# A four-layer graph network on one core: making the first elements and the matrix of the order statistics while the attention ends, moving the transposes of its result, and taking one product off VectorE

## The chip, the core and the metric

The kernel runs on one core of a Trainium2 chip. A core has five engines that run their own instruction streams: TensorE for matrix products (PE in the profile, with its weight loads as PEld), VectorE (DVE), ScalarE (ACT), GpSimd (POOL) and SyncE (SP). SP, ACT and POOL also issue the transfers between the device's memory and the core's on-chip memory, SBUF. Products land in PSUM, a second on-chip memory of eight banks. Times are device microseconds (us) of one execution.

## The reference: four layers over sixteen graphs

The input is `x`, 16 graphs x 1024 nodes x 64 channels, an adjacency matrix `adj` of 1024 x 1024 per graph, and a node mask. Four layers follow each other; after each the layer's input is added and a layer norm over the channels taken:

```
x = layernorm(x + L0(x, adj))   # degree-normalized product with adj, leaky relu
x = layernorm(x + L1(x, adj))   # attention, 8 heads, scores plus gated adj
x = layernorm(x + L2(x, adj))   # order statistics over neighbours, then an MLP
x = layernorm(x + L3(x, adj))   # adj @ (x @ W) + b
```

Layer 2 is the unusual one. Each node keeps a pruned list of its neighbours, and for each of the 64 channels it needs the neighbours' values at the quantiles 0.25, 0.5 and 0.75 (interpolated between two ranks and weighted):

```
nd   = adj_d > 0                                    # pruned neighbours
vals = where(nd[..., None], x[:, None, :, :], inf)
s    = sort(vals, axis=2);  nv = nd.sum(2)
for tau, w in zip((0.25, 0.5, 0.75), (0.25, 0.5, 0.25)):
    pos = tau * max(nv - 1, 0);  lo, hi = floor(pos), ceil(pos)
    agg = agg + w * (s[lo] + (pos - lo) * (s[hi] - s[lo]))
y = relu((x + agg) @ W1 + b1) @ W2 + b2
```

## The kernel before

**Turns.** The graphs go in eight pairs; the two graphs' 64 channels together fill the 128 partitions. The main loop (L1205) has nine turns. Turn p holds, in this order:

1. Layer 0 of both graphs of pair p (`layer0`, L402), which also finds the pruned neighbours and stores them as a mask in the device's memory (`nd_d`). Between the two graphs stand the last two layers of pair p-2 (`ends`, L1193, which calls `layers23`, L1029).
2. The attention of pair p (`attention`, L471): 64 steps of scores, exponentials, transposes and weighted sums, limited by TensorE, and at the end the projections of the heads (L562) with normalizations. The result `x2` is stored (L644), transposed on TensorE (L649), copied by ScalarE (L650) and stored again as `x2T` (L651).
3. A sort of pair p-1, beside the attention (`middle`, which calls `sort`). Every channel's 1024 values are sorted by a bitonic network of 55 steps. A forward step is three VectorE instructions, a comparison and two exchanges (all recorded as L1117), and a store of the comparison's mask. A backward pass replays the masks and yields every node's rank; `words_of` (L1079) turns ranks into three small numbers for each node and channel (`rk`, `u_w`, `b_w`). The swaps are written at step 58 of the attention. The last backward ones are paced, each behind an instruction of the attention; the forward ones have no such bond.
4. The order statistics of pair p-1 (`quantiles`, L788). VectorE makes *elements* E from those numbers (`words`, L767 to L785): a power of two for each node, by the rank. TensorE multiplies them with the neighbour matrix `ndT` (`half_word`, L849), so that a *word* V holds, as bits, which ranks occur among the neighbours, and sums of them. A group of 4 channels needs three words of 1024 columns, each made as two halves of eight matmuls, one bank a half, which ScalarE copies out (L857). There are 16 such groups per graph. Then come 96 steps, one for every group and quantile of both graphs: a comparison on VectorE (L862), a one-hot of the block (L871), a pick of the word at that block (L880, two of 1.75 us a step, the largest item on VectorE) and its sum on TensorE. Each eight steps make a *unit*, whose picked words are searched for the k-th set bit by a chain of short dependent VectorE instructions (`kth_bit`, L694 to L763). The found positions then select values (`distances`, `least_values`, `sum_values`), and a product with the interpolation's weights (L929) ends the unit, with a store of its result (L930). After the last step come the last search and a tail, mostly on TensorE, for the last unit.

Turn 0 has no sort and no order statistics. Turn 8 has neither layer 0 nor attention: the last layers of pair 6, the sort and the order statistics of pair 7. The last layers of pair 7 follow.

**What sets the order.** A scheduler ("planner" below) orders each engine's instructions ahead of time. It goes by the order in which the program is written as priority, and it gives a free engine any instruction that is ready by its estimates. A chain written out in the program (`then`, `product`) fixes the order of TensorE's matmuls in the attention and after the first words; some instructions (`behind`) are tied to others by hand. VectorE's stream has no such chain over the stages, so instructions of one stage can stand between those of another.

**Space.** SBUF is handed out in pools, from the left end or from the right end of a partition. A pool's tiles can only be written when the tiles that lay at that place before have been used for the last time. Beside the attention, the left end holds its data (`nat`, `att`), and the right end the sort's: `keys` at bytes 217056 to 229344 and `srt` at 201376 to 217056. The order statistics have three pools, `kb`, `qe` and `qn`, from byte 33088 up to 229088, so they lie over both the attention's and the sort's space. The elements, the matrix, `lim`, `V`, `lt` and `m` are in `qe`; the results and values (`vals`) in `qn`. The next turn's keys (L1169, loaded from `x2T`) lie at the right end again.

**The seams.** The matrix of the first graph is loaded by eight transfers on SP at the head of the order statistics, and there the first six elements are made, ahead of the first two groups' words, whose matmuls are outside the written-out chain.

Of the kernel before, what the change touches and what calls it, by code (L numbers as in the profile page):

```python
# [13 lines left out]
F32 = mybir.dt.float32  # L14
# [11 lines left out]
P = 128  # L26
N = 1024
# [83 lines left out]
def gnn_kernel(ctx: ExitStack, tc: tile.TileContext, a: dict, out: bass.AP):  # L111
# [100 lines left out]
    def bank(shape, dtype=F32):  # L212
        return ps1.tile(shape, dtype, name="bank")
# [257 lines left out]
    def attention(nat, ip, graphs, wqkv, x2, beside):  # L471

# [3 lines left out]
        with (tc.tile_pool(name="att", bufs=2, reuse_waits="tile") as att,  # L476
# [120 lines left out]
            for st, (gr, hp, nh, k4) in enumerate(steps):  # L597
                at = 8 * hp + 4 * nh + k4
                if k4 % 2 == 0:
                    pT = [[att1.tile([P, 4, 256], F32, name="pT", bufs=8) for mh in range(2)] for h in range(2)]  # L600
                scores_of(st + 1)
                if at == 2:
                    values(gr, 3)
                transposes(exps.pop(st), pT, k4 % 2)
                exponentials(exps.get(st + 1, ()))

                next(parts, None)
                if at == 0:
                    for _ in parts:
                        pass  # L610
                if k4 % 2:
                    for _ in parts:
                        pass
                    parts = weighted(gr, hp, 2 * nh + k4 // 2, pT)
                if at == 1:
                    for k in range(3):
                        values(gr, k)
                if gr is g1 and 2 <= at < 6:
                    heads(g0, at - 2)
                if st == BESIDE:  # L620
# [21 lines left out]
            for k in range(2, 4):  # L642
                heads(g1, k)
            nc.gpsimd.dma_start(x2_d[ds(ip * P, P)], x2)  # L644
            x2T = att1.tile([P, N], F32, name="t_pr")
            for hf in range(2):
                ps = bank([P, 4, P])
# [137 lines left out]
                nc.vector.tensor_tensor(Ev[w], Ev[1], over_t(b_w[w]), ALU.mult)  # L785
        return E

    def quantiles(ip, rk, u_w, b_w):  # L788

# [11 lines left out]
        with ExitStack() as es:  # L801
# [5 lines left out]
            class Graph(SimpleNamespace):  # L807
                pass

            graphs = [Graph(bb=bb, r=slice(bb * C, (bb + 1) * C), bd={}, base={}, V={}, E={}) for bb in range(2)]  # L810

            def load_matrix(gr):
                gr.ndT = qe.tile([P, NB, N], F8, name="ndT", bufs=2)
                for k in range(NB):
                    nc.sync.dma_start(gr.ndT[:, k, :].bitcast(U8), nd_d[gr.bb][ds(ip * P, P), k, :])
# [29 lines left out]

            def product(*args, **kw):
                then(nc.tensor.matmul(*args, **kw))  # L847

            def half_word(gr, g, w, hf, matmul):  # L849

# [71 lines left out]
            def sum_values(u, s):  # L922
                gr, g, q = u.pairs[s]
                for t in range(4):
                    product(u.acc[32 * t:32 * t + 32, :], bonesf[:, s, :], u.vals[s][t],
                            start=False, stop=(s == U8N - 1), tile_position=(0, 32 * t))
                if s == U8N - 1:
                    res = qn.tile([P, 512], F32, name="vals", bufs=5)
                    nc.vector.tensor_tensor(res, u.acc, gr.cf[u.n % 3], ALU.mult)  # L929
                    nc.gpsimd.dma_start(agg_d[gr.bb][:, u.n, :], res)  # L930

            picked = None
# [6 lines left out]
            todo = [(k, ws) for k in range(len(groups)) for ws in ([0], [1, 2])]  # L939
            made = used = 0  # L940

            def elements():

                nonlocal made
                k, ws = todo.pop(0)
                gr, g = groups[k]
                gr.E.setdefault(g, []).extend(words(qe, gr.bb * G + g, ws, rk, u_w, b_w))
                made += len(ws)

            def more_elements():  # L950
# [251 lines left out]

    for p in range(B // 2 + 1):  # L1205
        with double_banks(), ExitStack() as es:
            if p >= 1:
                keys = es.enter_context(tc.tile_pool(name="keys", bufs=1, reuse_waits="tile", side="right"))
                key = sort_keys(keys, p - 1)
            last = ends(p - 2) if p >= 2 else iter(())  # L1210
            if p < B // 2:
                nat = es.enter_context(tc.tile_pool(name="nat", bufs=1, reuse_waits="tile"))
                x2 = nat.tile([P, NB, 2, C], F32, name="x2")
                graphs = [Graph(bb=bb, x1=nat.tile(NODES, F32, name=f"x1_{bb}")) for bb in range(2)]
                adj = [nat.tile([P, N], F32, name=f"adj{k}") for k in range(NB)]
                wqkv = twice(nat, "wqkv", a["WqkvT"], 3 * H * C)
                with tc.tile_pool(name="l0", bufs=1, reuse_waits="tile") as l0:
                    tables = place_tables(l0)
                    for gr in graphs:
                        gr.adj = list(adj)  # L1220
                        layer0(l0, tables, p, gr.bb, None if gr.bb else adj, gr.x1)
                        if gr.bb == 0:
                            for part in (keys_of, gates, queries_of):
                                part(gr, nat, lambda i: None)
                            for k in range(NB):
                                gated(gr, k)
                            for _ in last:
                                pass
            for _ in last:
                pass  # L1230
            if p >= 1:
                srt = es.enter_context(tc.tile_pool(name="srt", bufs=1, reuse_waits="tile", side="right"))
            if p < B // 2:
                attention(nat, p, graphs, wqkv, x2, lambda pace: p and middle(keys, srt, key, pace))
            else:
                middle(keys, srt, key)
        if p >= 1:
# [34 lines left out]
```

## Time and profile before

| | |
|---|---|
| median of three runs | 13438.38 us (13429.95 to 13443.01) |
| the profiled execution's own time | 13445.01 us |
| its span | 13443.2 us |
| mean granted TensorE clock | 0.944 |
| busy: PE, PEld, DVE, ACT, POOL | 12131.7, 5255.1, 10695.0, 7227.6, 637.3 us |
| data moved | 510.91 MB, 38 GB/s on average |
| attention gives way to the order statistics at | 2854, 4503, 6148, 7796, 9441, 11089 us; first at 1209 |
| next turn begins at | 2205, 3851, 5500, 7143, 8791, 10437, 12085 us |
| turn without attention | 12085 to 12352 us, its order statistics to 13347 us |

The page of the profile gives each engine's busy time and share of the span. A row of an answer by stretches gives, for the window in its first column, each engine's busy microseconds with its number of instructions, the mean granted TensorE clock (1.00 is full speed), the share of time in which the transfer engines were busy, and the data rate. A line of the order on an engine gives the start, the mean time of one, the engine, the line of the program, the operation, `out<-in` with shapes and types, and how many stand in a row; in brackets the idle time before it and what ended that.

The turns repeat at about 1646 us, so one of them stands for six. By the stretches, the attention and the steps of the order statistics each fill their bounding engine, and what is idle lies at the seams between them. Transfers are a small share of time except at the turn's begin, in layer 0.

### The profile page before, as it was taken

The numbers are of one execution on the slowest core, as the hardware profiler recorded it, in microseconds if no ns is written. First come the engines' busy times: TensorE is split into PE (matmuls) and PEld (weight loads), VectorE is DVE, ScalarE is ACT, GpSimd is POOL, SyncE is SP. The second block draws the span as 40 slices with busy tenths as digits, with TensorE's granted clock in tenths as the row PEclk, the third lists the DMA queues.
The fourth block names the chain that finished last, engine by engine and source line by source line (L and its number), as shares of the span: only waits on it lengthen the run. The fifth ranks groups of instructions, "written<-read, shape, count | busy, mean of one in ns | idle before, by whom it ended". The sixth has DMA issues, their size and how long they took to land. (4 is left out here: it accounts for less than half of the span.)

```text
span 13443.2 us, 216369 instructions
## 1 busy us (share of the span) xinstructions
PE 12131.7 (90%) x85551; PEld 5255.1 (39%) x85632; DVE 10695.0 (80%) x18827; ACT 7227.6 (54%) x13164; POOL 637.3 (5%) x956
## 2 busy tenths in 40 slices
PE   7898997989979899798997989979899799993998
PEld 4554332543325433353333633336333353331332
DVE  3588887778877788777886788867888778978885
ACT  5665554655536555365553755536455465551553
POOL 0000000000000000000000010000100001000000
PEclk9999998999989999899998999989999899996999
DMA  2120003100031000310003100041000310002001
GB/s 78 68 64 19 5 5 102 60 18 5 6 119 43 16 6 5 126 38 14 5 5 132 32 14 5 5 134 38 6 5 27 113 36 6 8 23 76 4 5 44
DMA packets 356376, 510.91 MB, mean 38 GB/s; under 512 B 124448, under 2 KB 279584, under 8 KB 353312
## 3 DMA queue, kind: packets, MB, share of 16 engines
q1 hardware_dynamic: 288656, 368.00, 8.6%
q10 hardware_dynamic: 33040, 86.88, 2.0%
q0 software_dynamic: 33664, 42.19, 1.2%
q8 instruction: 673, 11.03, 0.3%
q14 instruction: 343, 2.81, 0.1%
HBM read 380.32 MB, written 116.59 MB: 37 GB/s over the span
## 5 line engine op out<-in xcount | busy, mean ns | idle before, releaser
L880 DVE TENSOR_TENSOR m<-V,oh 128x3072 bf16<-128x3072 bf16 x1536 | 2639.4, 1752 | 290.9 <-PE wps L847 266.1
L847 PE MATMUL bank<-ndT,E 128*128 128x512 fp8e4 x11904 | 2751.4, 381 | 7.6
L910 ACT ACTIVATE vals<-bank 128x512 f32<-128x512 f32 x3072 | 1592.6, 602 | 1398.6 <-PE bank L847 1396.6
L516 DVE CUSTOM_DVE_ANT_0 s<-banks,adj 128x1024 f32<-128x1024 f32 x1024 | 1214.3, 1221 | 799.2 <-PE banks L509 795.6
L857 ACT ACTIVATE V<-bank 128x512 uint16<-128x512 f32 x1536 | 912.5, 597 | 1734.4 <-PE bank L847 1645.7
L847 PEld LDWEIGHTS <-E 128*128 128x128 bf16 x11904 | 1118.1, 98 | 1798.2 <-issue 561.1
L871 ACT CAST oh<-bank 128x512 f16<-128x512 f32 x3072 | 1577.2, 601 | 314.7 <-PE bank L847 313.8
L847 PE MATMUL bank<-oh,bd 128*128 128x512 f16 x6144 | 1482.7, 385 | 0.0
L535 ACT COPY pT<-bank 128x512 f32<-128x512 f32 x1536 | 800.8, 594 | 790.8 <-PE bank L531 790.6
L524 ACT ACTIVATE s<-s,mx 128x1024 f32<-128x1024 f32 x1024 | 1176.7, 1161 | 71.8 <-DVE mx L516 69.2
L509 PE MATMUL banks<-kT,qT 64*128 64x512 f32 x4096 | 1088.8, 623 | 68.2 <-DVE mx L516 38.0
L862 DVE TENSOR_TENSOR lt<-V,lim 128x2048 bf16<-128x2048 uint16 x768 | 937.0, 1220 | 238.1 <-PE bank L847 236.6
L531 PEld LDWEIGHTS bank<-ident,s 128*128 128x128 f32 x8192 | 886.0, 141 | 400.7 <-issue 290.1
L531 PE MATMUL bank<-ident,s 128*128 128x128 f32 x8192 | 1017.6, 278 | 0.5 <-DVE pT L537 0.5
L545 PE MATMUL bank<-pT,v 128*64 128x256 f32 x8192 | 1000.1, 387 | 0.0
L847 PEld LDWEIGHTS <-bd 128*128 128x128 f16 x6144 | 543.1, 99 | 893.3 <-issue 360.4
L847 PE MATMUL bank<-lt,dif 128*128 128x512 bf16 x3072 | 819.9, 384 | 60.9 <-DVE lt L862 48.2
L847 PE MATMUL acc<-vals,bonesf 128*32 128x512 f32 x6144 | 849.4, 603 | 0.0
L847 PE MATMUL bank<-r,pen 32*128 32x512 f16 x6144 | 489.5, 386 | 243.3 <-DVE r L763 229.3
L847 PE MATMUL wps<-m,tonesb 128*32 128x512 bf16 x9216 | 644.4, 384 | 66.8 <-DVE m L880 66.7
L545 PEld LDWEIGHTS bank<-pT,v 128*64 128x64 f32 x8192 | 546.6, 137 | 309.5 <-issue 44.9
L847 PE MATMUL acc<-oh,base 128*32 128x512 f16 x9216 | 642.1, 384 | 0.0
(251 smaller groups left out, 13301.2 us busy)
## 6 DMA issues: line engine op xcount, KB each, us to landing
at<-in_adjT SPq DMA_DIRECT2D x256, 512.0 KB, 5.2
masks_d<-mask SPq DMA_DIRECT2D x440, 128.0 KB, 1.7
mask<-masks_d SPq DMA_DIRECT2D x440, 128.0 KB, 2.1
adj<-in_adj SPq DMA_DIRECT2D x96, 512.0 KB, 5.1
ad<-in_adj ACTq DMA_DIRECT2D x64, 512.0 KB, 4.0
agg_d<-vals POOLq DMA_DIRECT2D x96, 256.0 KB, 2.3
agg<-agg_d ACTq DMA_DIRECT2D x16, 1536.0 KB, 6.9
nd_d<-nd SPq DMA_DIRECT2D x128, 128.0 KB, 2.0
```

Of the source, the lines that this page charges most:

```text
L509: then(nc.tensor.matmul(ss[h][:, hf * 512:(hf + 1) * 512], gr.qk[hp, 0][HALF[h], k * P:(k + 1) * P], gr.qk[hp, 1][HALF[h], hf * 512:(hf + ...
L516: last = nc.vector.tensor_tensor_reduce(s, ss[h], gr.adj[k], -1.0, 3.0e38, ALU.add, ALU.min, mx)
L524: then_act(nc.scalar.activation(s, s, AF.Exp, bias=mx, scale=-1.0, accum_out=sm))
L531: then(nc.tensor.transpose(ps[:, m, :], exps[h][0][:, (4 * mh + m) * P:(4 * mh + m + 1) * P], ident))
L535: then_act(nc.scalar.copy(dst, ps))
L545: then(nc.tensor.matmul(po[HALF[h]], gr.v[:, 4 * mh + m, (2 * hp + h) * C:(2 * hp + h + 1) * C], pT[h][mh][:, m, :], start=(mh == 0 and m ...
L847: then(nc.tensor.matmul(*args, **kw))
L857: nc.scalar.activation(gr.V[g][:, w, cols], ps, AF.Copy, bias=OFF)
L862: nc.vector.tensor_tensor(u.lt, gr.V[g][:, None, 0, :].to_broadcast([P, 2, N]), gr.lim[q], ALU.is_lt)
L871: nc.scalar.copy(oh[:, kk, cols], ps)
L880: picked = nc.vector.tensor_tensor(u.m[kk], gr.V[g].bitcast(BF), u.oh[s][:, kk, None, :].to_broadcast([P, NW, N]), ALU.mult)
L910: nc.scalar.activation(vals[t], ys[t], AF.Relu)
```

## The change

Three things are edited.

- **Elements and matrix.** A function `lead` now loads the first graph's neighbour matrix and makes the first six elements. It is called by a function `ahead`, which the attention runs just before its last heads; in the turn without an attention it runs after the sort. `ahead` first gives back the sort's two pools and opens a pool `el` at the right end in their place, with room for one matrix (8 KB a partition) and all seven buffers of elements (2 KB each), 22.5 KB in all. All later elements are made in this pool too. It is open until the order statistics end. Their own pools now end near byte 206,560, and hold only the second graph's matrix.
- **Transposes.** From the second pair on, the attention stops after the store of `x2`. The transposes are made in the steps 5 and 7 of the order statistics: `transposed_half` loads half of `x2` back from the device's memory (SP), transposes four blocks in TensorE's written-out order, copies them on ScalarE and stores half of `x2T` (POOL).
- **Last product.** For the last unit of a pair, ScalarE copies the sum out of PSUM, and GpSimd multiplies it by the weights. All other units keep the product on VectorE.

```diff
@@ attention @@
                     elif gr is g0:
                         project(g1, 0, nh)
+            ahead()
 
             next(parts)
             for k in range(2):
...
             nc.gpsimd.dma_start(x2_d[ds(ip * P, P)], x2)
+            if ip:
+                return
             x2T = att1.tile([P, N], F32, name="t_pr")
...
+    def lead(el, ip):
+
+        graphs = [SimpleNamespace(bb=bb, r=slice(bb * C, (bb + 1) * C), bd={}, base={}, V={}, E={}) for bb in range(2)]
+        load_matrix(el, ip, graphs[0])
+        for g in range(2):
+            for ws in ([0], [1, 2]):
+                graphs[0].E.setdefault(g, []).extend(words(el, g, ws, rk, u_w, b_w))
+        return el, graphs
+
+    def load_matrix(pool, ip, gr):
+        gr.ndT = pool.tile([P, NB, N], F8, name="ndT")
+        for k in range(NB):
+            nc.sync.dma_start(gr.ndT[:, k, :].bitcast(U8), nd_d[gr.bb][ds(ip * P, P), k, :])
+
+    def quantiles(ip, rk, u_w, b_w, led, after):
...
+            def transposed_half(hf):
+
+                xs = qn.tile([P, 4, P], F32, name="vals", bufs=5)
+                nc.sync.dma_start(xs, x2_d[ds(after * P, P), 4 * hf:4 * hf + 4].rearrange("p k b c -> p k (b c)"))
+                ps = bank([P, 4, P])
+                for k in range(4):
+                    then(nc.tensor.transpose(ps[:, k, :], xs[:, k, :], ident))
+                xT = qn.tile([P, 4, P], F32, name="vals", bufs=5)
+                nc.scalar.copy(xT, ps)
+                nc.gpsimd.dma_start(x2T_d[ds(after * P, P), hf * 512:(hf + 1) * 512], xT.rearrange("p k n -> p (k n)"))
...
                 if s == U8N - 1:
                     res = qn.tile([P, 512], F32, name="vals", bufs=5)
-                    nc.vector.tensor_tensor(res, u.acc, gr.cf[u.n % 3], ALU.mult)
+                    if u is units[-1]:
+
+                        total = qn.tile([P, 512], F32, name="vals", bufs=5)
+                        nc.scalar.copy(total, u.acc)
+                        nc.gpsimd.tensor_tensor(res, total, gr.cf[u.n % 3], ALU.mult)
+                    else:
+                        nc.vector.tensor_tensor(res, u.acc, gr.cf[u.n % 3], ALU.mult)
                     nc.gpsimd.dma_start(agg_d[gr.bb][:, u.n, :], res)
...
-            load_matrix(graphs[0])
-            with tc.high_priority():
-                while made < 2 * NW:
-                    elements()
+            load_least(graphs[0])
             more_words(2 * NW, nc.tensor.matmul)
...
                 if i == 3 * NQ:
-                    load_matrix(graphs[1])
+                    load_matrix(qe, ip, graphs[1])
+                    load_least(graphs[1])
...
+                if i in (5, 7) and after is not None:
+                    transposed_half(i // 2 - 2)
...
@@ main loop @@
     for p in range(B // 2 + 1):
-        with double_banks(), ExitStack() as es:
+        with ExitStack() as over:
+            with double_banks(), ExitStack() as es:
+                right = es.enter_context(ExitStack())
+                if p >= 1:
+                    keys = right.enter_context(tc.tile_pool(name="keys", bufs=1, reuse_waits="tile", side="right"))
+                    key = sort_keys(keys, p - 1)
...
+                def ahead():
+                    nonlocal led
+                    if p:
+                        right.close()
+                        led = lead(over.enter_context(tc.tile_pool(name="el", bufs=1, reuse_waits="tile", side="right")), p - 1)
+
+                if p < B // 2:
+                    attention(nat, p, graphs, wqkv, x2, lambda pace: p and middle(keys, srt, key, pace), ahead)
+                else:
+                    middle(keys, srt, key)
+                    ahead()
             if p >= 1:
-            quantiles(p - 1, rk, u_w, b_w)
+                quantiles(p - 1, rk, u_w, b_w, led, p if p < B // 2 else None)
```

`load_least` is the second half of the former `load_matrix`: the twelve POOL loads of the table `bv`, unchanged.

More of the change, by code (lines that the diff above doesn't have):

```diff
@@ L469, in gated, with attention @@
                                 op0=ALU.mult, op1=ALU.mult)
-    def attention(nat, ip, graphs, wqkv, x2, beside):
+    def attention(nat, ip, graphs, wqkv, x2, beside, ahead):
         pace = []
@@ L786, in words @@
         return E
-    def quantiles(ip, rk, u_w, b_w):
+    def lead(el, ip):
[10 more added lines that the diff above has]
+    def quantiles(ip, rk, u_w, b_w, led, after):
         with ExitStack() as es:
@@ L805, in quantiles, with load_least @@
             psw = es.enter_context(tc.tile_pool(name="psw", bufs=1, space=PSUM, reuse_waits="tile"))
[L807 to L815, printed above, removed]
+            el, graphs = led
+            def load_least(gr):
                 gr.bv = qe.tile([P, G, 3], F16, name="bv", bufs=2)
@@ L938, in quantiles @@
             halves = iter([(k, w, hf) for k in range(len(groups)) for w in range(NW) for hf in range(2)])
-            todo = [(k, ws) for k in range(len(groups)) for ws in ([0], [1, 2])]
-            made = used = 0
+            todo = [(k, ws) for k in range(2, len(groups)) for ws in ([0], [1, 2])]
+            made, used = 2 * NW, 0
             def elements():
@@ L946, in elements @@
                 gr, g = groups[k]
-                gr.E.setdefault(g, []).extend(words(qe, gr.bb * G + g, ws, rk, u_w, b_w))
+                gr.E.setdefault(g, []).extend(words(el, gr.bb * G + g, ws, rk, u_w, b_w))
                 made += len(ws)
@@ L1201, in ends @@
                 yield
+    led = None
     for p in range(B // 2 + 1):
-        with double_banks(), ExitStack() as es:
-            if p >= 1:
[L1208 to L1236, printed above, removed]
@@ L1237, in gnn_kernel @@
-        if p >= 1:
-            quantiles(p - 1, rk, u_w, b_w)
+        with ExitStack() as over:
[4 more added lines that the diff above has]
+                    key = sort_keys(keys, p - 1)
+                last = ends(p - 2) if p >= 2 else iter(())
+                if p < B // 2:
+                    nat = es.enter_context(tc.tile_pool(name="nat", bufs=1, reuse_waits="tile"))
+                    x2 = nat.tile([P, NB, 2, C], F32, name="x2")
+                    graphs = [Graph(bb=bb, x1=nat.tile(NODES, F32, name=f"x1_{bb}")) for bb in range(2)]
+                    adj = [nat.tile([P, N], F32, name=f"adj{k}") for k in range(NB)]
+                    wqkv = twice(nat, "wqkv", a["WqkvT"], 3 * H * C)
+                    with tc.tile_pool(name="l0", bufs=1, reuse_waits="tile") as l0:
+                        tables = place_tables(l0)
+                        for gr in graphs:
+                            gr.adj = list(adj)
+                            layer0(l0, tables, p, gr.bb, None if gr.bb else adj, gr.x1)
+                            if gr.bb == 0:
+                                for part in (keys_of, gates, queries_of):
+                                    part(gr, nat, lambda i: None)
+                                for k in range(NB):
+                                    gated(gr, k)
+                                for _ in last:
+                                    pass
+                for _ in last:
+                    pass
+                if p >= 1:
+                    srt = right.enter_context(tc.tile_pool(name="srt", bufs=1, reuse_waits="tile", side="right"))
+                def ahead():
[3 more added lines that the diff above has]
+                        led = lead(over.enter_context(tc.tile_pool(name="el", bufs=1, reuse_waits="tile", side="right")), p - 1)
+                if p < B // 2:
+                    attention(nat, p, graphs, wqkv, x2, lambda pace: p and middle(keys, srt, key, pace), ahead)
+                else:
+                    middle(keys, srt, key)
+                    ahead()
+            if p >= 1:
+                quantiles(p - 1, rk, u_w, b_w, led, p if p < B // 2 else None)
```

## The prediction

> **What bounds the kernel now.** I read the page first, then busy time by stretches of one pair's turn, then the order on TensorE and VectorE at the two seams between stages. All windows are from the turn that ends about 5500 us; the other full turns repeat it.
>
> ```profile
> PE 12131.7 (90%) x85551; PEld 5255.1 (39%) x85632; DVE 10695.0 (80%) x18827; ACT 7227.6 (54%) x13164; POOL 637.3 (5%) x956
> ```
>
> ```profile
> core 0: us, PE busy (x) PEld busy (x) DVE busy (x) ACT busy (x) POOL busy (x), PEclk, DMA share, GB/s
> 4480.00:4494.00 14.00, 13.28 (x176) 10.72 (x175) 8.94 (x25) 2.23 (x4) 0.00 (x0) 1.00 0.01 2
> 4494.00:4504.00 10.00, 2.15 (x8) 1.39 (x8) 9.39 (x34) 1.38 (x3) 0.58 (x1) 0.62 0.01 5
> 4504.00:4518.00 14.00, 13.95 (x51) 5.74 (x52) 7.63 (x13) 3.42 (x6) 13.83 (x22) 0.78 0.28 73
> 4531.00:4636.00 105.00, 76.12 (x422) 29.51 (x419) 99.46 (x138) 44.73 (x82) 12.92 (x24) 0.90 0.02 3
> 5431.00:5460.00 29.00, 20.16 (x184) 7.16 (x182) 24.49 (x61) 9.60 (x17) 0.00 (x0) 0.92 0.12 29
> 5460.00:5500.00 40.00, 38.71 (x320) 12.68 (x312) 1.28 (x4) 19.17 (x37) 0.80 (x2) 0.93 0.53 188
> 5500.00:5512.00 12.00, 0.39 (x2) 0.40 (x3) 3.55 (x6) 1.01 (x2) 0.83 (x2) 0.64 0.97 314
> 5512.00:5720.00 208.00, 144.62 (x800) 66.92 (x810) 171.76 (x438) 67.11 (x105) 11.35 (x8) 0.80 0.46 151
> 12085.00:12352.00 267.00, 54.66 (x208) 23.04 (x208) 232.38 (x525) 7.96 (x13) 16.44 (x26) 0.58 0.35 109
> ```
>
> TensorE is full except at the seams. First seam: 2.15 us of work in the 10 us before the order statistics. Second: 12 us with nothing, after a tail (5460 to 5500) in which VectorE in turn has nothing. From 4531 to 4636 VectorE is the bound (99.46 of 105), so TensorE work put there is covered. In the turn without an attention (12085 to 12352) VectorE sorts alone.
>
> ```profile
> 4492.78 1.06 PE L562 MATMUL bank<-wp,o 64*128 64x64 f32 x16
> 4501.04 2.15 PE L649 MATMUL bank<-ident,x 128*128 128x128 f32 x8 [7.20 <-DVE x L277]
> 4504.05 1.46 PE L856 MATMUL bank<-ndT,E 128*128 128x512 fp8e4 x3 [0.86 <-DVE E L781]
> ...
> 5459.27 0.42 DVE L763 TENSOR_TENSOR r<-pos 128x512 f16<-128x512 uint16 x1
> 5498.75 0.69 DVE L929 TENSOR_TENSOR vals<-acc,cf 128x512 f32<-128x512 f32 x1 [38.46 <-PE acc L847]
> 5508.45 0.69 DVE L1117 TENSOR_TENSOR mask<-key 128x512 f16<-128x512 f32 x1 [8.68 <-DMA key<-x2T_d]
> ```
>
> TensorE waits 7.20 us for the last normalization, makes the transposes, then waits for the first elements. VectorE waits 38.46 us at the last product; then come 8.68 us for the sort's keys, whose load can be issued only when that product lets the space go.
>
> **First seam, seven times.** Removed there: eight transposes (2.15 us on PE), two ACT copies of 0.59 and a POOL store of 0.53 us. The matrix's eight SP loads (0.43 us to issue, 3.6 to land, by their line) now wait for the sort's last tiles, 4462.6, and land near 4470. Ten element instructions (4 x 0.68 + 2 x 0.42 + 2 x 0.67 and two more of 0.68: 6.3 us) are ready to run from 4462.6; VectorE idles 3.17, 2.73, 1.36, 0.70 and 4.84 us before its next instructions up to 4485.5, 12.8 us in all, so they fit without holding the heads. Without that cover they are 6.3 us. So the words can follow the last head matmul at 4493.84 where they now start at 4504.05: 10.2 us. What is late next: their ACT copies still stand behind the last square root (4500.0 to 4500.3), but four PSUM banks hold four of the six half words (2.25 us each, 9 us), so nothing stops. The counts, limits and first comparison follow the words, so the first pick moves with them. Bounds: 0 (words stay behind ACT) and 13 (they also run at full clock; 0.78 now). I take 10: 7 x 10 = **-70**.
>
> **Transposes in the order statistics.** Two loads on SP, eight transposes (2.15 us), two copies (1.2 us), two stores on POOL between the lookup loads, near the sixth and eighth step. PE has 29 us of slack in that window, and ACT 60: 0. If the cover fails, TensorE in its ordered chain waits for bank and load, 2.2 to 5 us each, +35 in all.
>
> **The last product.** ACT copies the sum (0.6 us by the copies of a 128x512 bank), POOL multiplies. The nearest POOL row is L468, 1.13 us for 1024 elements, one input; I take 1.1, between 0.6 and 2.2. The store is a microsecond later; its reader is the second graph's load, some 60 us later. 0. The Trainium skill, "GPSIMD Engine Reference" (Elementwise), gives two-input work 2.6 cycles per element against one on VectorE; an estimate from that page for 512 elements at 1.2 GHz is 1.1 us. Against the move stands "SBUF — State Buffer" (SBUF: two separate sides): a GpSimd op and a VectorE op with two SBUF inputs lock each other out. The trace has such a case, L372 at 5558.39:
>
> ```profile
> 5558.39 1.26 DVE L372 TENSOR_SCALAR rem<-rem,m 128x1024 bf16<-128x1024 f16 x1
> ...
> 5560.59 0.47 DVE L372 TENSOR_SCALAR rem<-rem,m 128x1024 bf16<-128x1024 f16 x1
> ```
>
> Held 0.8 us while POOL runs L468. By the page one swap would wait up to a multiply, 7 x 1.1 = 8 us off the path; the sum stays.
>
> **The second seam: an unnamed consequence.** The first elements now live where the sort's keys will, at the right end, and their last use is the last word (5389.2). The next keys need only x2T, now stored early. So the key load (4.1 us undisturbed, by its line's minimum) can go near 5390 rather than at 5500.3, and the sort's 165 forward swaps (0.64 us each in a row) are ready from 5395. They are written in step 58 of the next attention, yet already run in layer 0: the planner gives a free engine any ready instruction. It does this between dependent instructions too:
>
> ```profile
> 5632.75 0.69 DVE L1054 TENSOR_TENSOR y<-bank,b_r 128x512 f32<-128x512 f32 x1 [2.43 <-PE bank L1052]
> 5633.36 0.68 DVE L1117 TENSOR_TENSOR key<-key 128x512 f32<-128x512 f32 x1
> 5633.96 0.69 DVE L1055 TENSOR_TENSOR y<-y,mask_f 128x512 f32<-128x512 f32 x1
> ```
>
> L1054 to L1055 takes 1.21 us; alone 0.72 (0.69 and a gap of 0.03), so a swap between costs 0.48. The tail on TensorE waits for the last search (the k-th bit, 5434.2 to 5459.7), a chain in which I count 38 dependent gaps, with 8 more in the search before it: 46 x 0.48 = 22 us, plus 1 for swaps that overrun a true gap. Bounds 0 (none put between) and 100 x 0.48 = 48 (also at picks and independent steps). I take 23, since in layer 0 every dependent gap had a swap: 7 x 23 = **+161**.
>
> Against it stand the swaps done ahead: 46, some 11 in 7 us of gaps, 60 in the 38 us tail; about 120 of 165. In layer 0, six times, 54 swaps now stand directly in front of another instruction (46 of them after 5545). About 45 fewer delays x 0.48 = 22 us, half on the path (the rest beside loads of the adjacency): -11, bounds -3 and -22: **-66**. At its front the keys no longer hold VectorE 8.7 us, but SP's loads of x and adjacency, issued inside the tail now, stand behind the swaps' mask stores; x lands 4 to 5 us after the tail: -4, bounds +5 and -9: **-24**. In the turn without an attention the backward half waits for the last layers' space: they end 12195.7, 7 earlier without swaps, so the backward half starts at about 12196 rather than 12241: -46, bounds -30 and -55. But there the matrix waits for the sort's end, 12352.3: +4. Together **-42**.
>
> **Sum:** -70 + 0 + 161 - 66 - 24 - 42 = -41. The profiled execution took 13445.0 (span 13443.2, 1.8 around it): 13404. The median of the runs is 6.6 lower: 13397. Faster or slower than no change is what lies outside 0.2%, 27 us.
>
> **Rivals.** (1) *The search is not delayed*: the keys land too late, or nothing is put between. For it: the 38.46 us gap alone takes 60 swaps. Against: 40 us lie between the last word and the last search. -41 - 161, with half the layer-0 gain lost (+30): 13266. (2) *Slower, by the search*: 100 swaps stand in the last searches and steps. For it: VectorE has only 4 us idle from 5396 to 5430, so every swap there delays a pick. 48 rather than 23 each: +175, 13572. It decides above 23 + 41/7 = 29 us per seam, 60 swaps. (3) *The words start no earlier*, because their banks or order hold them behind the last normalization: that part of the change doesn't do what it says. For it: today the elements start only after L277, though their inputs were ready at 4462.6. +70: 13467.
>
> **Chances.** Forecast 0.45 (own range 13330 to 13460), rival 1 0.2, rival 2 0.2, rival 3 0.15. In the forecast about 0.29 falls faster, 0.13 same, 0.03 slower; rival 1 all faster; rival 2 0.18 slower, 0.02 same; rival 3 0.08 slower, 0.06 same, 0.01 faster. Faster 0.50, same 0.21, slower 0.29. The range 13260 to 13540 leaves out the far halves of rivals 1 and 2.
>
> **What would show it.** First words within 2 us of the last L562, no L649 after the first pair's; key loads near 5390 in the turn; swaps between L750 and L759 and no 38 us gap on VectorE; the last search some 45 us long instead of 25; few swaps after the first 40 us of layer 0; the sort-only turn 40 us shorter. I am wrong if the search keeps its length, if the seam still shows 7 us, or if adjacency loads come so late that layer 0 grows.

## The result: 0.65% slower, where 0.3% faster was forecast

The changed kernel took 13530.66 us, the median of four runs (13502.50 to 13535.27), against 13437.22 for the kernel before (four runs, one more than in the table above). The ratio is 1.0065, with a 95% interval of 1.0048 to 1.0083. The prediction was 13397, with a chance of 0.5 for faster; of its four times the measured one is nearest to the second rival's (13572, "slower, by the search"). The profiled execution took 13535.27 us with a span of 13533.5, 90.3 more than the span before.

Stages can be compared to a tenth of a microsecond, since the turns repeat. The boundaries are TensorE's last product of the heads (L562), the first word (L849 of before), the first and the last pick, the end of the last search (L763), TensorE's last sum in the tail, and the next attention's first scores. A first number is the sum over all seven full turns (six for layer 0) in the kernel before, in us; the next is the same sum of the kernel after, less that. All go by the starts in the two traces, but for the last pick, which counts by its end:

| stage | before | after less before | predicted |
|---|---|---|---|
| last head product to first word | 73.4 | -72.0 | -70 for both rows |
| first word to first pick | 185.5 | -10.2 | |
| first to last pick | 6300.1 | +88.1 | part of the search's +161; transposes 0 |
| last pick to end of last search | 198.2 | +143.4 | +161, with the row above |
| tail | 269.3 | +2.5 | 0 |
| tail's end to next scores (layer 0 and last layers) | 1333.8 | -17.8 | -90 (-66 and -24) |
| turn without an attention, tail's end to first word | 270.0 | -42.5 | -42 |
| all other | | -1.2 | 0 |
| sum | | +90.3 | -41 |

Busy time by stretches of the kernel after, in the turn whose last pick ends at 5470; the columns are those of the rows shown of before. In order: the last search, the tail, layer 0's front up to the first propagation, the rest of layer 0, and the turn without an attention.

```profile
core 0: us, PE busy (x) PEld busy (x) DVE busy (x) ACT busy (x) POOL busy (x), PEclk, DMA share, GB/s
5470.00:5519.50 49.50, 20.59 (x172) 6.79 (x172) 49.43 (x109) 9.81 (x17) 0.54 (x1) 0.72 0.21 62
5519.50:5558.50 39.00, 38.91 (x320) 12.85 (x319) 34.92 (x56) 16.85 (x32) 0.00 (x0) 0.92 0.47 169
5558.50:5594.00 35.50, 7.33 (x31) 3.91 (x34) 31.57 (x56) 10.47 (x20) 1.74 (x2) 0.57 0.67 209
5594.00:5773.00 179.00, 132.81 (x770) 58.45 (x776) 68.40 (x265) 60.91 (x92) 9.35 (x8) 0.86 0.42 140
12214.00:12441.00 227.00, 54.97 (x213) 23.10 (x208) 157.12 (x401) 8.55 (x14) 17.44 (x26) 0.59 0.34 104
```

VectorE, idle for 38 us in the tail before, is now busy there and all through the search, which has the same work for TensorE (20.59 us now, 20.16 before) and takes 49.5 us instead of 29. Then TensorE is busy 7 of 35 us. The first seam did what was said. The order on TensorE after:

```profile
4529.47 3.79 PE L562 MATMUL bank<-wp,o 64*128 64x64 f32 x64
4533.19 7.08 PE L878 MATMUL bank<-ndT,E 128*128 128x512 fp8e4 x32
4540.81 3.61 PE L878 MATMUL bank<-ndT,E 128*128 128x512 fp8e4 x16 [0.54 <-ACT V L879]
```

The words follow the heads directly, and the one wait on ScalarE's copies is 0.54 us. In the last search, VectorE's order after:

```profile
5482.01 0.42 DVE L724 TENSOR_SCALAR S<-S 128x1024 uint16<-128x1024 uint16 x1
5482.34 0.68 DVE L1145 TENSOR_TENSOR mask<-key 128x512 f16<-128x512 f32 x1
5482.94 0.68 DVE L725 TENSOR_TENSOR S<-S,U 128x1024 uint16<-128x1024 uint16 x1
5483.55 0.69 DVE L1145 TENSOR_TENSOR key<-key 128x512 f32<-128x512 f32 x1
5484.15 0.42 DVE L726 TENSOR_SCALAR U<-S 128x1024 uint16<-128x1024 uint16 x1
5484.48 0.70 DVE L1145 TENSOR_TENSOR key<-key 128x512 f32<-128x512 f32 x1
```

In this stretch every gap of the chain holds a swap of the next sort (L1145 now). In each of the seven turns 25 swaps stand between the picks' last steps and 45 between the last pick and the search's end, 70 in all. The front of layer 0 is what the prediction did not see. SyncE's queue before (one line) and after, and VectorE's order after; in a line with several instructions (`x27`) the second number is the time from the start of the first to the end of the last:

```profile
5468.66 1.66 SPq L407 DMA_DIRECT2D x<-in_x  x2
```

```profile
5429.35 89.99 SPq L1171 DMA_DIRECT2D masks_d<-mask  x24
5519.76 4.05 SPq L424 DMA_DIRECT2D adj<-in_adj  x8
5524.82 51.87 SPq L1171 DMA_DIRECT2D masks_d<-mask  x27
5576.78 0.40 SPq L311 DMA_DIRECT2D place<-in_c_place  x1
5577.23 0.48 SPq L313 DMA_DIRECT2D identb<-in_c_idb  x1
5577.80 1.17 SPq L407 DMA_DIRECT2D x<-in_x  x2
```

```profile
5579.51 0.69 DVE L1145 TENSOR_TENSOR mask<-key 128x512 f16<-128x512 f32 x1
5582.41 0.20 DVE L315 TENSOR_SCALAR negidb<-identb 128x128 bf16<-128x128 bf16 x1 [2.21 <-DMA identb<-in_c_idb]
...
5583.83 0.68 DVE L410 TENSOR_TENSOR y<-x,bn_a 128x512 f32<-128x512 f32 x1
```

Twenty-seven mask stores, each waiting for its swap, stand ahead of the loads of layer 0's tables and of x, which go out 19 to 20 us after the tail's end (5557.9); before the change x's load went out some 30 us ahead of it (5498.1). TensorE's first propagation (`bank<-at,y`) comes 35 to 37 us after the tail in all six turns, where it came after 21.

### The profile page after: what moved, and what is told of

Same layout as the page of the kernel before. It is cut to its first block, busy times and chain, and to the rows that moved or that the text cites. A ratio compares the mean times of both kernels' runs of the same rounds, so it can differ in the third digit from the quotient of the medians.

```text
span 13533.5 us, 216467 instructions
## 1 busy us (share of the span) xinstructions
PE 12111.9 (89%) x85545; PEld 5230.5 (39%) x85632; DVE 10674.1 (79%) x18819; ACT 7239.0 (53%) x13172; POOL 642.8 (5%) x971
```

## The experiments

What was expected of each run, with its rival, stands ahead of its result. Times are medians; ratios are to the kernel before, run beside it.

**Swaps held behind the last search.** `searched` holds the last instruction of the last search made (`kth_bit`).

```diff
-        behind = chain([None] * (3 * STEPS), (p for p in pace for _ in range(PACE)))
+        behind = chain((searched + [None])[:1], [None] * (3 * STEPS - 1), (p for p in pace for _ in range(PACE)))
```

> The changed kernel, with the first forward swap of the next sort ordered behind the last instruction of the last search (on VectorE's own order, no new semaphore). Theory A (swaps made ready early stand between the dependent instructions of the last picks and the last search, each 0.4 to 0.7 us on the path): the last search goes back from 48.8 to 28.3 us and the last four steps lose their 10.4 us, 7 x 31 = -216. The swaps then fill the tail (about 60 of 165) and some 105 are left for layer 0 instead of 41; SyncE still has 26 mask stores in front of layer 0's first tables, so these are issued about 11 us after the tail (-7 each against the changed kernel, -42) while the extra swaps in layer 0 cost about 0.14 us each (+53). Sum about 13325, range 13260 to 13400. Theory B (the search is longer for another reason, such as the pools' new places or transfers, or the swaps' time comes back in full in layer 0): 13480 or more.

Measured: 13396.27 us, ratio 0.9967 (0.9955 to 0.9980). Theory A holds: the last search is 28.3 us long again (sum over the turns +0.1 to before), and the steps lose 57 of their 88 us. VectorE's order in the last search of this kernel:

```profile
5420.79 0.69 DVE L727 TENSOR_TENSOR S<-S,U 128x1024 uint16<-128x1024 uint16 x1
5421.52 0.43 DVE L728 TENSOR_SCALAR U<-S 128x1024 uint16<-128x1024 uint16 x1
5421.98 0.69 DVE L729 TENSOR_TENSOR S<-S,U 128x1024 uint16<-128x1024 uint16 x1
```

From one dependent instruction to the next, L727 to L728, takes 0.73 us here. In the kernel after, 5482.94 to 5484.15 (L725 to L726) takes 1.21 with one swap between. That is 0.48 a swap, as the prediction had it from layer 0. Seventy swaps cost 30.9 us a turn (10.4 in the last steps and 20.5 in the search), 0.44 each.

The time was still 71 us above what was expected. Three reasons make some 50 of it. The order held the comparison of the first step only, so its two exchanges still ran in the search of the unit before:

```profile
5379.98 0.69 DVE L1147 TENSOR_TENSOR key<-key 128x512 f32<-128x512 f32 x1
5380.58 0.68 DVE L762 TENSOR_TENSOR wb<-wb,U 128x1024 uint16<-128x1024 uint16 x1
...
5381.72 0.69 DVE L1147 TENSOR_TENSOR key<-key 128x512 f32<-128x512 f32 x1
```

They cost the picks some 2.5 us, in that turn and in the others: more than 0.48 apiece. That a comparison and the picks stand right behind them is the likely reason, but no run separates it. The front of layer 0 did not move: its first instruction on x still came 25 to 26 us after the tail's end, where 18 was expected. With some 115 swaps still to do after the tail, layer 0 and the last layers took 225 us, 5.7 more than in the kernel after. And the turn without an attention, with 105 swaps left behind its tail, kept 31 of the 42.5 us that it had gained.

**Mask stores on GpSimd.**

```diff
-            nc.sync.dma_start(masks_d[:, i, :], mask)
+            nc.gpsimd.dma_start(masks_d[:, i, :], mask)
```

> The changed kernel, with the stores of the forward swaps' masks issued by GpSimd instead of SyncE. Theory A2 (layer 0 begins late because SyncE's in-order stream has 27 mask stores, each waiting for its swap, in front of the loads of layer 0's tables and x): the loads go out at the end of the last search, x's first instruction comes back from 25 us after the tail to some 11 us, 6 x -14 = -83; the search stays at 48.8 us: about 13447, range 13420 to 13480. Theory B2 (the loads wait for space that the tail holds, since the pools have moved): the front stays at 20 us or more, 13510 to 13540.

Measured: 13487.88 us, ratio 1.0033 (1.0020 to 1.0046). Neither theory is right as it stood. SyncE's queue and VectorE's order in this kernel, in the turn whose tail ends at 5545.1:

```profile
5512.35 0.33 SPq L311 DMA_DIRECT2D place<-in_c_place  x1
5512.73 0.51 SPq L313 DMA_DIRECT2D identb<-in_c_idb  x1
5515.39 1.92 SPq L407 DMA_DIRECT2D x<-in_x  x2
```

```profile
5568.47 1.29 DVE L1145 TENSOR_TENSOR key<-key 128x512 f32<-128x512 f32 x2
5569.68 0.19 DVE L315 TENSOR_SCALAR negidb<-identb 128x128 bf16<-128x128 bf16 x1
5569.90 0.20 DVE L317 TENSOR_SCALAR noteye<-negidb 128x128 bf16<-128x128 bf16 x1
5570.01 0.68 DVE L410 TENSOR_TENSOR y<-x,bn_a 128x512 f32<-128x512 f32 x1
```

The loads of the tables and of x go out 30 us ahead of the tail's end, as before the change, so their space was free (B2 falls) and SyncE's queue had held them. Yet L410 stands 25 us after the tail, with no wait in front of it: it follows a run of swaps in VectorE's fixed order. GpSimd's queue shows a third stream:

```profile
5561.69 0.54 POOL L1171 DMA_DIRECT2D masks_d<-mask  x1 [1.39 <-DVE mask L1145]
5562.25 1.16 POOL L955 TENSOR_TENSOR vals<-vals,cf 128x512 f32<-128x512 f32 x1
5563.71 0.58 POOL L958 DMA_DIRECT2D agg_d<-vals  x1 [0.30 <-POOL vals L955]
```

The last product, moved to GpSimd by the change, now stands behind the mask stores: it starts 17 us after the tail's end in this turn, where it started after 1.3 in the kernel after. Three of layer 0's first four loads of the transposed adjacency (`at`) go out at 21 to 24 us, 0.06 to 0.27 us after the store of that product has landed, in all six turns. So three in-order streams held the same front, and freeing SyncE's showed the others. Layer 0 with the last layers took 210 us instead of 219; 7 of these 9 us were gained after the first propagation, with the swaps done by then, and 2.5 at the front.

**Both edits together.**

```diff
-        behind = chain([None] * (3 * STEPS), (p for p in pace for _ in range(PACE)))
+        behind = chain((searched + [None])[:1], [None] * (3 * STEPS - 1), (p for p in pace for _ in range(PACE)))
...
-            nc.sync.dma_start(masks_d[:, i, :], mask)
+            nc.gpsimd.dma_start(masks_d[:, i, :], mask)
```

> Both edits together: swaps behind the last search and their mask stores on GpSimd. If theories A and A2 hold and add: 13530 - 216 - 83 + 53 (more swaps left for layer 0) = 13284, range 13230 to 13350, faster than the kernel before by some 1.1%. If the swaps' time only moves: 13430 or more.

Measured: 13410.72 us, ratio 0.9979 (0.9969 to 0.9989). They do not add. L410 is again 26 to 27 us after the tail's end in VectorE's order, now with more swaps left behind it, and GpSimd's product again starts some 17 us after the tail's end.

**The first part alone** (elements and matrix ahead; transposes at the attention's end; product on VectorE).

```diff
-            if ip:
-                return
             x2T = att1.tile([P, N], F32, name="t_pr")
...
-                if i in (5, 7) and after is not None:
+                if False:
...
-                    if u is units[-1]:
...
+                    nc.vector.tensor_tensor(res, u.acc, gr.cf[u.n % 3], ALU.mult)
```

> The kernel before with the first part of the change alone: elements and matrix made while the attention ends; transposes stay at the attention's end, the last product on VectorE. If the early space for the keys comes from this part alone (theory A), the search is 48.8 us long here too; against the changed kernel the transposes in steps 5 and 7 are gone (-2 each), and cost at the first seam between 0 and 3 us: 13510 to 13540. Rival: it is the transposes' move or the product's that lets the keys come early; then the search is 28 us long and the time 13300 to 13380.

Measured: 13539.20 us, ratio 1.0077 (1.0062 to 1.0092). The early keys come from this part alone: the last search takes 48.8 us here too. But the seam hardly closes (-7.4 us in seven turns). The order on TensorE in this kernel:

```profile
4519.85 3.79 PE L562 MATMUL bank<-wp,o 64*128 64x64 f32 x64
4530.84 2.15 PE L650 MATMUL bank<-ident,x 128*128 128x128 f32 x8 [7.21 <-DVE x L277]
4532.79 2.77 PE L876 MATMUL bank<-ndT,E 128*128 128x512 fp8e4 x6
```

The elements are ready, and the words stand in order behind transposes that wait 7.21 us for the last normalization. Layer 0 with the last layers takes 211 us in this kernel, 8 less than in the changed one (219), and that takes back most of what the changed kernel's seam gains over this one. Why the two differ there was not tried.

**The second part alone** (transposes in steps 5 and 7 of the kernel before).

```diff
             nc.gpsimd.dma_start(x2_d[ds(ip * P, P)], x2)
+            if ip:
+                return
...
+                if i in (5, 7) and after is not None:
+                    transposed_half(i // 2 - 2)
```

> The kernel before with the second part of the change alone: transposes in steps 5 and 7 of the order statistics, elements and matrix as before. The run with the first part alone kept 9.4 of the seam's 10.5 us, since the first words stayed behind the transposes. If the seam needs both parts, elements still start behind the last normalization here and the seam stays near 10 us; the steps lose 1 to 2 us each: 13437 + 7 to 14 = about 13447, range 13430 to 13460. Rival: the transposes alone hold the seam: 7 x -9 + 12 = 13386, range 13370 to 13410.

Measured: 13465.75 us, ratio 1.0018 (1.0009 to 1.0028), a little above the range. The seam stays as it was; on TensorE:

```profile
4509.56 10.75 PE L869 MATMUL bank<-ndT,E 128*128 128x512 fp8e4 x41 [10.22 <-DVE E L783]
```

So the seam's 10.3 us need both parts: each of the two alone leaves the other's wait. The steps grow by 14.4 us in seven turns, which is the price of the transposes that the prediction put at nothing. The longer gap in this kernel and in the changed one opens between the steps 9 and 13 (counted from 0, as 5 and 7 are), beside the first search; which of the transposes' instructions makes it was not tried.

**Swaps in two parts.** `started` holds the first graph's L411. The first 45 swaps wait for the last search, with all three of the first step held, and the rest for L411. The first run also has the mask stores on GpSimd, the second leaves them on SyncE.

```diff
+        first = nc.vector.tensor_tensor(hn, hn, over_nodes(bn_b), ALU.add)
+        if bb == 0:
+            started[:] = [first]
...
+        behind = chain((searched * 3 or [None] * 3), [None] * 42, (started * 3 or [None] * 3), [None] * (3 * STEPS - 48), (p for p in pace for _ in range(PACE)))
```

> The changed kernel with the swaps in two parts: the first 45 ordered behind the last search (all three of the first step, not the first alone, which let two swaps through in the run before), the rest behind layer 0's second instruction on x (L411); mask stores on GpSimd. Theory C (layer 0 began late in the changed kernel and in the three held and moved runs because VectorE's fixed order has a run of swaps in front of layer 0's first instructions, 25 us after the tail, whichever queue issues the loads): layer 0's first instruction comes 0 to 8 us after the tail, the search and the last steps stay as before the change, each turn of layer 0 some 205 us instead of 222. Against the kernel before: seam -10.5, words -1.3, transposes +2.2, 7 times: -67; layer 0 6 x -17 = -102; sort-only turn -31 to -42. 13437 - 205 = 13235, range 13190 to 13330. Rival (the front is late because x or the adjacency lands late): front at 20 us or more, 13340 to 13400.

> The same with the mask stores left on SyncE, which has 15 of them in front of layer 0's loads: these then go out about 10 us before the tail's end instead of 30. Theory C: 13225 to 13330, no more than 5 us a turn above the other. Rival (SyncE's queue sets the front): 10 us a turn or more above it.

Measured: 13364.74 us with the stores on GpSimd, ratio 0.9942 (0.9927 to 0.9957), and 13335.53 us with them on SyncE, ratio 0.9918 (0.9904 to 0.9933). Theory C holds for the front: layer 0's first instruction on x comes at the tail's end (8 us ahead of it with GpSimd's stores, -0.7 to +2.4 us with SyncE's). SyncE's queue and VectorE's order with SyncE's stores, in the turn whose tail ends at 5464.5:

```profile
5432.04 29.52 SPq L1177 DMA_DIRECT2D masks_d<-mask  x15
5461.65 0.38 SPq L311 DMA_DIRECT2D place<-in_c_place  x1
5462.08 0.45 SPq L313 DMA_DIRECT2D identb<-in_c_idb  x1
5462.62 0.93 SPq L409 DMA_DIRECT2D x<-in_x  x2
```

```profile
5461.13 1.29 DVE L1151 TENSOR_TENSOR key<-key 128x512 f32<-128x512 f32 x2
5464.49 0.20 DVE L315 TENSOR_SCALAR negidb<-identb 128x128 bf16<-128x128 bf16 x1 [2.08 <-DMA identb<-in_c_idb]
5464.73 0.20 DVE L317 TENSOR_SCALAR noteye<-negidb 128x128 bf16<-128x128 bf16 x1
5466.07 1.48 DVE L412 TENSOR_TENSOR y<-x,bn_a 128x512 f32<-128x512 f32 x1 [1.15 <-DMA x<-in_x]
```

But the first propagation comes 22 to 24 us after the tail, and no earlier than before the change. The trace shows a new wait there:

```profile
5463.61 13.33 SPq L330 DMA_DIRECT2D at<-in_adjT  x4
5479.48 0.69 DVE L333 TENSOR_SCALAR nbt<-at 128x1024 bf16<-128x1024 f32 x1 [9.27 <-DMA at<-in_adjT]
```

The first of the four loads of the transposed adjacency goes out at once, the second 10 to 11 us after the tail's end, in each of the six turns 0.19 us after the store of the last result has landed; VectorE waits 9 to 12 us for it. In the kernel before, all four went out 21 to 26 us ahead of the tail's end. So their places are now held until that store is done: these loads, and neither VectorE's order nor SyncE's mask stores, keep the front at its old length here. Layer 0 is 218 us long with SyncE's stores, and not 205. With the stores on GpSimd it is 223, although x's loads go out earlier. GpSimd's queue in that kernel shows the stores mixed with the products on the adjacency (L472), each store waiting for its swap:

```profile
5529.95 0.54 POOL L1177 DMA_DIRECT2D masks_d<-mask  x1 [7.28 <-DVE mask L1151]
5536.15 0.54 POOL L1177 DMA_DIRECT2D masks_d<-mask  x1 [5.65 <-DVE mask L1151]
```

Whether that costs the 5 us, or the different order that the planner made, was not told apart.

**All swaps behind layer 0's second instruction.**

```diff
+        behind = chain((started * 3 or [None] * 3), [None] * (3 * STEPS - 3), (p for p in pace for _ in range(PACE)))
```

> The changed kernel with all swaps ordered behind layer 0's second instruction on x, so that none stands in the search or in the tail: what the change does without its early swaps. 7 x -9.6 (seam, words, transposes) = -67, the sort-only turn -25 to -42, layer 0 with all 165 swaps again, 213 to 222 us instead of 222 (-54 to 0): 13437 - 92 - 0 to 54 = 13290 to 13350, say 13320. It tells whether swaps in the tail are worth anything: against the split they cost 10 to 17 us a turn by theory C; by the rival (swaps fill idle time wherever they stand) 0.

Measured: 13401.96 us, ratio 0.9966 (0.9955 to 0.9978), 50 above the expected range. 30 of it come from the seventh turn, whose next turn has no layer 0, so that nothing held its swaps there: steps and search grew as in the kernel after. The rest is in layer 0, 225 us long. VectorE's order in this kernel, tail's end at 5466.6:

```profile
5445.84 0.69 DVE L413 TENSOR_TENSOR y<-y,bn_b 128x512 f32<-128x512 f32 x1
5446.45 0.68 DVE L1149 TENSOR_TENSOR mask<-key 128x512 f16<-128x512 f32 x1
5467.21 0.69 DVE L333 TENSOR_SCALAR nbt<-at 128x1024 bf16<-128x1024 f32 x1 [20.08 <-PE acc L862]
```

Layer 0's first instructions run 21 us ahead of the tail's end, and then VectorE stands 20.08 us at L333 until TensorE's last sum: one swap has passed and all others stand behind it. The order statistics' pools now end 22.5 KB further left, so other tiles lie over one another. The wait says that L333's tile now takes the place of values which the tail's last sums read. That the shift is the reason is likely, but no run with the pools at their old places tested it. The adjacency loads wait here too, until 10 us after the tail. So an early start of layer 0 buys nothing here, and swaps in the tail are worth about 7 us a turn (225 against 218).

**The third part undone in the best version.**

```diff
-                    if u is units[-1]:
...
+                    nc.vector.tensor_tensor(res, u.acc, gr.cf[u.n % 3], ALU.mult)
```

> The version with the swaps in two parts and the mask stores on SyncE, with the third part of the change undone: the last product on VectorE again. In that version three of the four first loads of the transposed adjacency go out 11 us after the tail, behind a tile of values that the last product and its store hold. If GpSimd's slower product (1.2 us after a copy of 0.6) is part of that, these loads come some 2 us earlier and with them layer 0: 6 x -2 = -12, and the last pair's end 0.8 us earlier: 13322, range 13305 to 13345. Rival: the third part is worth nothing either way, 13335 within 15. Second rival: VectorE's product stands in front of layer 0's first instructions and costs them about 1 us each: 13342.

Measured: 13322.35 us, ratio 0.9911 (0.9894 to 0.9927). The estimate was met, and in the trace the second adjacency load goes out 8.3 to 10.1 us after the tail's end instead of 9.9 to 11.1, again 0.19 us after the store has landed; layer 0 is 1.5 us shorter a turn. But the intervals of this and the run with GpSimd's product overlap nearly whole, and the first rival's range holds the time too, so what the third part costs, 13 us by the medians, is not settled. The two kernels with the swaps in two parts and SyncE's stores are faster than both the kernel before (0.8 to 0.9%) and the changed one.

## Why the prediction was wrong, step by step

- **First seam (-70): right.** -72.0 for the seam, and -10.2 as the words then ran at full clock (granted clock 1.00 there, 0.78 before), which was the upper bound's reason. That both parts are needed was not said in the working, which took each wait as gone; the two runs of one part show that each alone leaves the seam within 1.1 us of its old length.
- **Transposes (0): too low.** "PE has 29 us of slack" was so, but the steps grew by some 2 us a turn: 14.4 in the run of this part alone, 15 to 17 in the two best versions.
- **Last product (0): the price about right, the effect not settled.** GpSimd's product took 1.15 to 1.60 us, 1.1 was taken. The lock of which the Trainium skill tells, "SBUF — State Buffer" (SBUF: two separate sides), agrees with the trace: in each of the seven full turns one swap beside that product took 1.5 to 1.65 us instead of 0.69. The row that the prediction shows for it is another case: L372 is a `tensor_scalar` with one tensor read from SBUF, not two. That the delay lies off the path is not shown: the swap stands in the row of swaps that VectorE's order has in front of layer 0. Undoing this part in the best version gave 13 us by the medians, within the noise.
- **Search (+161): the mechanism was right, the number of swaps too small.** The price of one was 0.48 us, as taken from layer 0. The prediction counted 38 gaps in the last search and 8 in the one before, 46 swaps; there were 70, with 25 among the picks of the last steps, which it had kept for the upper bound only. Measured: 30.9 us a turn, 216 in all: 20.5 in the last search, where some 19 were counted, and 10.4 in the steps, against 4. This is the second rival's mechanism. It set its own point of decision at 29 us a turn, or 60 swaps, and that was passed. That the time came near the rival's is partly luck: the rival had 100 swaps and 336 us here, and kept layer 0's -90.
- **Layer 0 (-66 and -24): the step that failed most.** After the first propagation layer 0 was 18 us a turn shorter (183 against 201; predicted 11, bounds 3 and 22), so fewer swaps did help. But the front was sized at -4, with +5 as its bound, and it was +15. The working named SyncE's stores and then let x land "4 to 5 us after the tail"; it never counted the 27 stores in front, 52 us of queue. And it did not ask what VectorE's fixed order has in front of L410. With both out of the way (swaps in two parts) the first propagation came at 22 to 24 us instead of 35 to 37. Together -17.8 instead of -90.
- **Turn without an attention (-42): right,** -42.5, and as worked out: its backward half starts 113 us after the tail instead of 157, and the first word waits 3 us for the matrix.

The failed terms add up: swaps +55, layer 0 +72, transposes +15, against -12 at the words. That is +130 on -41.

## What to carry to other kernels

When a change frees space or data early, list every instruction that becomes ready, and look at each in-order stream it will enter: compute placed in the gaps of a chain of short dependent instructions costs its own time less the gap (0.48 us of 0.69 here), and a transfer that waits for such an instruction holds all that its queue has behind it, and on GpSimd the arithmetic too (a product that starts 16 us later). Bound such work on both sides, by what it must not delay and by what must come first after it: the change with that bound was 1.4% faster than without. Where two waits end in the same place, removing one of them shows little; test the pair.

## What the runs showed that was not expected

- Two swaps that slipped into the search of the unit before the last delayed the picks by some 2.5 us, 1.2 us each, and not 0.48.
- Layer 0's front was never shorter than some 21 us after the tail: with its first instruction at +25 to +28, +11.5 to +12, 0 and -21 to -22 us, the first propagation came at 33 to 37, 21, 22 to 24 and 22 to 23 us. The nearly equal last three have different reasons. In the kernel before VectorE waits for the keys (8.68 us); in the other two the adjacency loads wait for the last result's store. Giving these loads a place that the store does not hold was not tried.
- With the mask stores on GpSimd, busy 5% of the span before, the two-part version was 29 us slower by the medians than with them on SyncE.
